# A graph layer on one core: node work on VectorE queued behind the turning of edges from block 24 on

## The chip, the cores and the metric

The kernel runs on one core of a Trainium2 chip. The core has a matmul engine (TensorE, PE in the profile, with its weight loads as PEld), VectorE (DVE), ScalarE (ACT), GpSimd (POOL) and SyncE (SP). Each engine works off its own queue in order, and they wait for each other through semaphores. The metric is the time of one execution on the device in microseconds, the median of several runs. Lower is better.

## The reference

The kernel computes one layer of a graph network over 8,192 nodes with 256 channels and 131,072 edges with 64 attributes each. Edges come sorted by their destination `dst`.

```python
ea = edge_attr @ w_e + b_e
msg = relu(x[src] + ea)                       # one row of x gathered for every edge
agg = segment_sum(msg, dst, num_segments=N)
t = x + agg
h_local = bn1(relu(t @ w1 + b1) @ w2 + b2 + x)
# attention inside groups of 32 nodes, 4 heads of 64
h_attn = bn2(attention(x) @ out_w.T + out_b + x)
out = h_local + h_attn
out = bn3(out + relu(out @ m_w1 + m_b1) @ m_w2 + m_b2)
result = layernorm(x + out)
```

All arithmetic is in 32-bit floats.

## The kernel before

Edges are cut into 128 blocks of 1,024, nodes into 16 chunks of 512. A block takes these steps:

- `gather` has GpSimd fetch the block's rows of x in eight indirect transfers of 128 rows (L217, tile `xs`, six buffers). Six blocks take one of the eight from SyncE instead (`FETCHED`, tile `xf`). From block 20 on the rows come from `xb`, a copy of x with the edge bias added.
- `edge_transpose` (L288) turns the block's edge attributes on VectorE with a 32x32 transpose: `ea` to `eaT`. This is "the turning of edges". `eaT` has two buffers, so the turning for block b+2 can begin only when the matmuls of block b have read theirs.
- `edge_products` multiplies `eaT` by the edge weights into the PSUM tile `pe` (two buffers of two banks each).
- `edge_messages` adds `xs` to `pe` on VectorE (L348) and applies the relu on ScalarE (L352), both in `xs`. The additions wait for the gathers.
- `edge_hot` builds on VectorE the 0/1 matrix `oh` (L363) that says which destination each edge has.
- `pair_sums` or `some_sums` sum the messages by destination with matmuls into `pw`; `edge_sums` copies them to `ws` (ScalarE) and builds a second 0/1 matrix `oh2` (VectorE, L402); `edge_place` multiplies the two into `l` and adds the result to the nodes' `xT` (VectorE, L422).

The node work of a chunk comes from three generators. `attention_front` makes the queries and keys. `attention_back` makes the values (`vn`, L609), the scores, then the softmax on VectorE: `mx` (L635), the subtraction (L638), an exponential on ScalarE (L639), the sum `sm` (L642), its reciprocal (L643), the scaling (L645) and four transposes into `bd` (L649). Then come matmuls that read `bd`. `dense` does the two feed-forward parts with VectorE steps in `hA` (L672, L701) and `zT` (L719), then the final normalisation in `y`, `st`, `mv`, `rstd` (L732 to L744). The last chunks use `dense_rows` (L761 on).

What sets the order: TensorE's order is the order of the program text throughout (`manual_schedule`). VectorE's and ScalarE's are written out the same way up to block 24 (`NV`), where `stated[0]` becomes false. From then on the framework's scheduler orders these two by its own estimate of when each instruction is ready, and `tc.issue_after(ins)` adds one rule: what is traced inside it on the engine of `ins` stands behind `ins` in that engine's queue. It adds no wait for `ins` to finish. From block 104 (`TAIL`) on, the text is produced by a small planner with due times, and it takes blocks one by one.

The gathers run under `hold_fetches`: each gather also waits for a matmul that the plan puts about 10 us (`AHEAD`) before it, at 1.254 us for each gather.

In the kernel before, two functions queue their work behind the newest turning: the additions of `edge_messages` and the comparisons of `edge_hot`, by way of `turned_at`:

Of the kernel before, what the change touches and what calls it, by code (L numbers as in the profile page):

```python
# [12 lines left out]
AF = mybir.ActivationFunctionType  # L13
ALU = mybir.AluOpType
# [5 lines left out]
P = 128  # L20
N, C, E, ED, H, NPG = 8192, 256, 131072, 64, 4, 32
# [3 lines left out]
NB = E // BE  # L25
NH = 4
WN = P // NH
TJ = BE // NH // P
TB = NH * TJ
QR = 32  # L30
EQ = P // QR
# [12 lines left out]
FETCHED = [44, 54, 64, 76, 86, 98]  # L44
# [40 lines left out]
def gnn_kernel(ctx: ExitStack, tc: tile.TileContext, x, src, dst, edge_attr, w, out):  # L85
    nc = tc.nc
# [16 lines left out]
    iota_n = const.tile([P, WB], FP, name="iota_n")  # L103
# [15 lines left out]
    rel = const.tile([P, NB, TB], FP, name="rel")  # L119
# [14 lines left out]
    for v in VECS:  # L134
        n = w[v].shape[0] // P
# [92 lines left out]
    xf_of = {}  # L228
# [48 lines left out]
    stated = [True]  # L277

    def between():
        for do in spots:  # L280
            do()

    turned_at = [None]

    def edge_transpose(b):
        ea, g0 = ea_of[b // 2], b % 2 * NH * EQ
        eaT = eaT_of[b] = epool.tile([P, NH * EQ, QR], FP, name="eaT", tag="eaT", bufs=2)
        turned_at[0] = nc.vector.transpose(eaT, ea[:, QR:].rearrange("p (g d) -> p g d", d=ED)[:, g0 : g0 + NH * EQ, :QR]).ins  # L288


    pe_of, msg_of, oh_of, pw_of, newest = {}, {}, {}, {}, {}
# [21 lines left out]
    def next_edges(b):  # L313
        if b < NB:
            edge_transpose(b)
        ahead = 2 + (b >= 24)
        while loaded[0] < min(b + ahead, NB - 1):
            loaded[0] += 1
            load_edges(loaded[0])
        fetch_rows(b - 2)  # L320

    def edge_messages(b, pairs=range(0, NH, 2), of_pair=range(2)):

        xs = xs_of[b]
        if b not in msg_of:
            msg_of[b] = xs
        msg = msg_of[b]
        n = 2 if b < NB - 1 else 1
        with ExitStack() as behind:
            if not stated[0]:  # L330
                behind.enter_context(tc.issue_after(turned_at[0]))
            for h in pairs:
                pe = pe_of[b, h]
                for u in of_pair[::n]:
                    hs = slice(h + u, h + u + n)
                    if h + u + n == NH and b in FETCHED:
                        for us, js, rows in (
                            (slice(0, 2), slice(0, TJ - 1), xs[:, h:]), (slice(0, 1), slice(TJ - 1, TJ), xs[:, h:]),
                            (slice(1, 2), slice(TJ - 1, TJ), xf_of[b]),
                        ):  # L340
                            rows = rows[:, None, None, :] if rows is xf_of[b] else rows[:, us, js].rearrange("p u i c -> p i u c")
                            nc.vector.tensor_add(
                                msg[:, h:][:, us, js].rearrange("p u i c -> p i u c"), pe[:, js, us, :], rows
                            )
                        nc.scalar.activation(msg[:, hs], msg[:, hs], AF.Relu)
                        continue
                    for js in [slice(0, TJ)] if n == 2 or h + u < NH - 1 else [slice(j, j + 1) for j in range(TJ)]:
                        nc.vector.tensor_add(  # L348
                            msg[:, hs, js].rearrange("p u i c -> p i u c"), pe[:, js, u : u + n, :],
                            xs[:, hs, js].rearrange("p u i c -> p i u c"),  # L350
                        )
                        nc.scalar.activation(msg[:, hs, js], msg[:, hs, js], AF.Relu)  # L352
        between()

    def edge_hot(b):

        oh = oh_of[b] = epool.tile([P, TB, WN], FP, name="oh", tag="oh", bufs=2)
        with ExitStack() as behind:
            if not stated[0]:
                behind.enter_context(tc.issue_after(turned_at[0]))  # L360
            for t0 in range(0, TB, TB // 2):
                ts = slice(t0, t0 + TB // 2)
                nc.vector.tensor_tensor(  # L363
                    oh[:, ts],
                    iota_n[:, None, :WN].to_broadcast([P, TB // 2, WN]),
                    rel[:, b, ts, None].to_broadcast([P, TB // 2, WN]),
                    ALU.is_equal,
                )

    def group_sums(pw, i, b, turns):  # L370
        for h, j in turns:
# [58 lines left out]
    with tc.tile_pool(name="setup", bufs=1) as sp:  # L430
# [16 lines left out]
        for v in VECS:  # L447
            r, n = col[v]
# [14 lines left out]
        for b in range(2):  # L463
            edge_transpose(b)
            load_edges(b + 2)
# [3 lines left out]
        edge_products(0, (2,))  # L469
        next_edges(2)  # L470
        edge_messages(0)


# [450 lines left out]
    with tc.manual_schedule(engines={PE}):  # L924
# [39 lines left out]
        for i, c, a, z in (  # L964
# [20 lines left out]
        b = 0  # L985
        while b < TAIL:
# [24 lines left out]
            if stated[0]:  # L1011
                for h in range(0, NH, 2) if b else ():
                    edge_products(b, (h,))
                    edge_messages(b, (h,))
# [17 lines left out]
                copy_some(2)  # L1032
# [6 lines left out]
            else:  # L1039
# [24 lines left out]
        p, m = [b, 0], [b, 0]  # L1064
# [10 lines left out]
        while l < NB:  # L1075
# [56 lines left out]
            elif t >= times[2]:  # L1132
                i, k = p
# [17 lines left out]
    with tc.If(wide > 0):  # L1151
        with tc.tile_pool(name="gen", bufs=1) as pool, tc.tile_pool(name="gen_ps", bufs=1, space=PSUM) as ps_pool:
# [11 lines left out]
            with tc.For_i(0, E, P * TE) as e0:  # L1164
                ea = pool.tile([P, TE, ED], FP, name="gea")
# [7 lines left out]
                xs = pool.tile([P, TE, C], FP, name="gxs")  # L1173
# [7 lines left out]
                for j in range(TE):  # L1181
# [89 lines left out]
```

## Time and profile before

| what | value |
|---|---|
| median of three runs | 1311.12 us (1310.87 to 1316.0) |
| profiled execution: time, span | 1310.63 us, 1308.9 us |
| granted TensorE clock in it | 0.966 |
| busy: PE, DVE, ACT, POOL | 1200.1, 792.5, 581.6, 971.1 us |
| turnings of edges, 128x512 | 128, 701 ns each |
| additions 128x1024 | 248, 1217 ns each |
| transposes into `bd`, 32x512 | 64, 701 ns each |

A row of the timeline view gives start, length, engine, line, operation, tiles, form and count; in brackets how long the engine stood idle before it, and what ended that. A row of the windows view gives the stretch, its length, the busy time of each engine shown with the number of its instructions, the granted TensorE clock, the share of the transfer engines and GB/s.

### The profile page before, as it was taken

What the parts mean: (1) busy time and instruction counts of PE and PEld (TensorE: products, weight loads), DVE (VectorE), ACT (ScalarE), POOL (GpSimd) and SP (SyncE); (2) the same over time, 40 slices, a digit from 0 to 9 for tenths busy, and PEclk for the clock granted to TensorE, in tenths of its full rate; (3) what the DMA queues carried; (4) which work ended last, traced back from release to release, by engine and by line L of the source; (5) the groups of instructions that cost most, each with busy time, mean ns of one, the idle gap of its engine ahead of it and who ended that gap; (6) DMA issues with size and microseconds to landing.
All of it is one profiled execution on the core that took longest, in us unless ns stands there. A gap on an engine that the chain in (4) does not pass through costs nothing.

```text
span 1308.9 us, 23368 instructions
## 1 busy us (share of the span) xinstructions
PE 1200.1 (92%) x7671; PEld 722.8 (55%) x7671; DVE 792.5 (61%) x1643; ACT 581.6 (44%) x840; POOL 971.1 (74%) x1026
## 2 busy tenths in 40 slices
PE   4997999899979989798998979979889999999997
PEld 3564556555546545555555545545455655556576
DVE  6676856647446565474746638346565765666563
ACT  3443534445526354352544426425245544545343
POOL 6777777777777777777777777777777777777772
PEclk9998999999999989899999989989989999999999
DMA  8999987767768657667687765866777775777642
GB/s 235 290 298 331 285 218 171 166 174 172 187 151 202 155 152 183 163 159 184 155 187 182 175 167 145 190 162 175 183 186 170 189 182 138 202 160 183 150 133 62
DMA packets 146298, 240.53 MB, mean 184 GB/s; under 512 B 24606, under 2 KB 109756, under 8 KB 145404
## 3 DMA queue, kind: packets, MB, share of 16 engines
q0 software_dynamic: 48864, 133.50, 38.1%
q1 hardware_dynamic: 88828, 98.15, 32.4%
q10 hardware_dynamic: 8480, 7.35, 1.9%
q8 instruction: 62, 1.02, 0.3%
q14 instruction: 64, 0.52, 0.1%
HBM read 222.13 MB, written 16.78 MB: 183 GB/s over the span
## 4 chain that ended last, share of the span: by engine, by line
PE 76%; DMA 9%; issue 5%; DVE 4%; POOL 3%; ACT 1%; SPq 0%; DVEq 0%; POOLq 0%; ACTq 0%
PE at L174 38%; PE pe L174 20%; PE pw L174 9%; PE l L174 5%; DMA xs<-xb,srci 4%; POOL xs L217 3%; DVE xs L348 2%; DMA xn<-in_x_dram 2%; DMA xs<-in_x_dram,srci 1%; PE at L775 1%; PE at L178 1%; DMA ea<-in_edge_attr_dram 1%; PE at L726 1%; ACT xs L352 1%; DMA last_src<-in_src_dram 0%
## 5 line engine op out<-in xcount | busy, mean ns | idle before, releaser
L217 POOL DMA_INDIRECT xs<-xb,srci x858 | 815.4, 950 | 262.3 <-issue 181.4
L352 ACT ACTIVATE xs<-xs 128x1024 f32<-128x1024 f32 (+2 forms) x253 | 263.0, 1045 | 434.0 <-DVE xs L348 357.8
L348 DVE TENSOR_TENSOR xs<-pe,xs 128x1024 f32<-128x1024 f32 (+2 forms) x253 | 300.0, 1204 | 211.1 <-PE pe L174 105.4
L174 PE MATMUL pe<-we,eaT 64*128 64x256 f32 x2048 | 271.1, 401 | 10.1 <-DVE xs L348 8.7
L174 PEld LDWEIGHTS pe<-we,eaT 64*128 64x128 f32 x2048 | 196.1, 194 | 108.5 <-issue 66.3
L174 PE MATMUL pw<-xs,oh 128*32 128x256 f32 x2048 | 142.9, 395 | 32.4 <-issue 20.2
L217 POOL DMA_INDIRECT xs<-in_x_dram,srci x144 | 138.6, 962 | 45.2 <-issue 29.3
L174 PEld LDWEIGHTS pw<-xs,oh 128*32 128x32 f32 x2048 | 61.0, 111 | 113.7 <-issue 54.1
L174 PE MATMUL at<-xT,inT 128*128 128x512 f32 x256 | 121.2, 600 | 1.9 <-ACT xT L578 1.9
L174 PE MATMUL at<-hA,mw 128*128 128x512 f32 (+1 forms) x256 | 114.4, 573 | 0.0
L288 DVE STREAM_TRANSPOSE eaT<-ea 128x512 f32<-128x512 f32 x128 | 89.6, 701 | 36.2 <-PE pe L174 31.4
L174 PE MATMUL at<-m,mw 128*128 128x512 f32 (+1 forms) x256 | 108.9, 570 | 0.0
L174 PEld LDWEIGHTS l<-oh,ws 128*128 128x128 f32 x512 | 74.7, 197 | 20.3 <-issue 16.4
L422 DVE TENSOR_TENSOR xT<-l,xT 128x352 f32<-128x352 f32 (+14 forms) x107 | 43.2, 427 | 70.4 <-PE l L174 70.3
L174 PE MATMUL l<-oh,ws 128*128 128x160 f32 (+4 forms) x512 | 85.8, 308 | 0.0
L174 PEld LDWEIGHTS at<-xT,inT 128*128 128x128 f32 x256 | 47.0, 190 | 60.5 <-issue 50.5
L174 PEld LDWEIGHTS at<-m,mw 128*128 128x128 f32 x256 | 47.0, 190 | 46.5 <-issue 42.2
L707 ACT ACTIVATE m<-at,vec 128x512 f32<-128x512 f32 (+1 forms) x64 | 41.8, 655 | 66.3 <-PE at L174 66.2
L174 PEld LDWEIGHTS at<-hA,mw 128*128 128x128 f32 x256 | 46.1, 190 | 44.0 <-issue 41.0
L591 ACT ACTIVATE qk<-at,vec 128x512 f32<-128x512 f32 x64 | 43.8, 685 | 52.9 <-PE at L174 52.5
L174 PE MATMUL pe<-qk 64*128 64x128 f32 x512 | 42.3, 321 | 23.2 <-DVE xs L348 23.2
L174 PE MATMUL at<-oT,outT 128*128 128x512 f32 x128 | 61.5, 604 | 0.3 <-ACT oT L664 0.3
(157 smaller groups left out, 1282.6 us busy)
## 6 DMA issues: line engine op xcount, KB each, us to landing
ea<-in_edge_attr_dram SPq DMA_DIRECT2D x252, 256.0 KB
xs<-xb,srci POOLq DMA_INDIRECT x858
xf<-xb SPq DMA_DIRECT2D x768, 1.0 KB
xn<-in_x_dram ACTq DMA_DIRECT2D x14, 512.0 KB
out_dram<-y SPq DMA_DIRECT2D x14, 512.0 KB
xp<-in_x_dram SPq DMA_DIRECT2D x10, 512.0 KB
xb<-xp SPq DMA_DIRECT2D x10, 512.0 KB
xp<-in_x_dram SPq DMA_DIRECT2D x3, 1024.0 KB
```

Source lines behind the costliest of these rows:

```text
L174: mark(ps, nc.tensor.matmul(ps, *args, **kw).ins)
L178: ins = nc.tensor.transpose(ps, *args).ins
L217: nc.gpsimd.indirect_dma_start(out=xs[:, h, j, :], out_offset=None, in_=x if b < NX else xb[:, :], in_offset=bass.IndirectOffsetOnAxis(ap= ...
L288: turned_at[0] = nc.vector.transpose(eaT, ea[:, QR:].rearrange("p (g d) -> p g d", d=ED)[:, g0 : g0 + NH * EQ, :QR]).ins
L348: nc.vector.tensor_add(msg[:, hs, js].rearrange("p u i c -> p i u c"), pe[:, js, u : u + n, :], xs[:, hs, js].rearrange("p u i c -> p i u c"),
L352: nc.scalar.activation(msg[:, hs, js], msg[:, hs, js], AF.Relu)
L422: newest["xT"] = nc.vector.tensor_add(xT, l2[:, :, a - n : z - n], xT).ins
L591: nc.scalar.activation(qk[:, o, :], ps, AF.Identity, bias=v_("in_b", o))
L707: newest["relu"] = nc.scalar.activation(m1[:, o, :], layer(mw1, KC, o, hA), AF.Relu, bias=v_("m_b1", o)).ins
L726: nc.tensor.transpose(ps[:wt, t - t2, k * P : (k + 1) * P], zT[:, k, t * P : t * P + wt], ident)
L775: nc.tensor.matmul(ps[i], wt[:, k, o * P : (o + 1) * P], act[:, k, :], start=(k == 0), stop=(k == nk - 1))
```

## The change

`edge_transpose` now opens an `issue_after` context on its own instruction and leaves it open until the next turning is traced (the last block's turning opens none). All that is traced on VectorE between two turnings is queued behind the first: the comparisons and additions as before, and now `oh2`, `xT`, `hA`, `vn`, `zT`, the softmax and the normalisation too. The two inner contexts of `edge_messages` and `edge_hot` go away.

```diff
-    turned_at = [None]
+    behind_turn = ctx.enter_context(ExitStack())

     def edge_transpose(b):
         ea, g0 = ea_of[b // 2], b % 2 * NH * EQ
         eaT = eaT_of[b] = epool.tile([P, NH * EQ, QR], FP, name="eaT", tag="eaT", bufs=2)
-        turned_at[0] = nc.vector.transpose(eaT, ea[:, QR:]...).ins
+        ins = nc.vector.transpose(eaT, ea[:, QR:]...).ins
+        behind_turn.close()
+        if not stated[0] and b < NB - 1:
+            behind_turn.enter_context(tc.issue_after(ins))
...
     def edge_messages(b, pairs=range(0, NH, 2), of_pair=range(2)):
-        with ExitStack() as behind:
-            if not stated[0]:
-                behind.enter_context(tc.issue_after(turned_at[0]))
-            for h in pairs:
...
+        for h in pairs:
...
     def edge_hot(b):
-        with ExitStack() as behind:
-            if not stated[0]:
-                behind.enter_context(tc.issue_after(turned_at[0]))
-            for t0 in range(0, TB, TB // 2):
...
+        for t0 in range(0, TB, TB // 2):
```

No instruction is added or removed. The rows of PE, POOL and SP stand in the same order before and after; VectorE's rows move, and with them some of ScalarE's. The new file is three lines shorter above most of the code, so that its line numbers are three lower there.

The first place is VectorE's queue past block 104, at the softmax of the chunk before the last. Before, this stood there (`eaT` is a turning, the additions are `xs<-pe,xs`, `oh` alone are the comparisons, `oh` with a number is `oh2`):

```order
L719 TENSOR_TENSOR zT<-at,zT 128x512
L635 TENSOR_REDUCE mx<-pr 128x16
L638 TENSOR_TENSOR pr<-pr,mx 128x128 x4
L642 TENSOR_REDUCE sm<-pr 128x16
L719 TENSOR_TENSOR zT<-at,zT 128x512
L643 RECIPROCAL sm<-sm 128x16
L645 TENSOR_TENSOR pr<-pr,sm 128x128 x4
L649 STREAM_TRANSPOSE bd<-pr 32x16x32 x4
L288 STREAM_TRANSPOSE eaT<-ea 128x512
L363 TENSOR_TENSOR oh<-iota_n,rel 128x128 x2
L422 TENSOR_TENSOR xT<-l_10516,xT 128x2x144
L348 TENSOR_TENSOR xs<-pe,xs 128x2x2x256 x2
```

The whole softmax stood ahead of the turning. Now, at the same place of the same queue, where the normalisation of another chunk (`y`, `st`, `mv`) is met as well:

```order
L288 STREAM_TRANSPOSE eaT<-ea 128x512
L360 TENSOR_TENSOR oh<-iota_n,rel 128x128 x2
L419 TENSOR_TENSOR xT<-l_10516,xT 128x2x144
L348 TENSOR_TENSOR xs<-pe,xs 128x2x2x256 x2
L632 TENSOR_REDUCE mx<-pr 128x16
L729 TENSOR_TENSOR y<-at,xn 128x512
L635 TENSOR_TENSOR pr<-pr,mx 128x128 x4
L729 TENSOR_TENSOR y<-at,xn 128x512
L731 BN_STATS st<-y 128x6
L639 TENSOR_REDUCE sm<-pr 128x16
L732 BN_AGGR mv<-st 128x2
L731 BN_STATS st<-y 128x6
```

The softmax stands behind the turning, its comparisons, an addition to `xT` and two additions of messages, and it alternates with the normalisation; after these rows come the reciprocal, the scaling, two more `st` and two more `mv`, and then the four `bd<-pr`.

The second place is the softmax of the last chunk, some 60 us later in VectorE's queue. Before:

```order
L635 TENSOR_REDUCE mx<-pr 128x16
L638 TENSOR_TENSOR pr<-pr,mx 128x128 x4
L288 STREAM_TRANSPOSE eaT<-ea 128x512
L363 TENSOR_TENSOR oh<-iota_n,rel 128x128 x2
L422 TENSOR_TENSOR xT<-l_10987,xT 128x2x128
L348 TENSOR_TENSOR xs<-pe,xs 128x2x2x256 x2
L642 TENSOR_REDUCE sm<-pr 128x16
L719 TENSOR_TENSOR zT<-at,zT 128x512
L643 RECIPROCAL sm<-sm 128x16
L402 TENSOR_SCALAR oh_11042<-iota_n,wrow 128x128
L645 TENSOR_TENSOR pr<-pr,sm 128x128 x4
L649 STREAM_TRANSPOSE bd<-pr 32x16x32 x4
```

Its first half filled the time ahead of the turning. After the change, from the comparisons on:

```order
L360 TENSOR_TENSOR oh<-iota_n,rel 128x128 x2
L419 TENSOR_TENSOR xT<-l_10987,xT 128x2x128
L348 TENSOR_TENSOR xs<-pe,xs 128x2x2x256 x2
L632 TENSOR_REDUCE mx<-pr 128x16
L716 TENSOR_TENSOR zT<-at,zT 128x512
L635 TENSOR_TENSOR pr<-pr,mx 128x128 x4
L399 TENSOR_SCALAR oh_11042<-iota_n,wrow 128x128
L716 TENSOR_TENSOR zT<-at,zT 128x512
L639 TENSOR_REDUCE sm<-pr 128x16
L640 RECIPROCAL sm<-sm 128x16
L642 TENSOR_TENSOR pr<-pr,sm 128x128 x4
L646 STREAM_TRANSPOSE bd<-pr 32x16x32 x4
```

All of it stands behind the additions, and its second half also behind the second `zT`, which stood behind `bd` before.

The third place is another 60 us on, at a block's `oh2`, the tile `oh_11593`. Before, in VectorE's queue:

```order
L363 TENSOR_TENSOR oh<-iota_n,rel 128x128 x2
L402 TENSOR_SCALAR oh_11593<-iota_n,wrow 128x112
L732 TENSOR_TENSOR y<-at,xn 128x512
L764 TENSOR_TENSOR xc<-xn,c3row 128x256
L734 BN_STATS st<-y 128x6 x2
L735 BN_AGGR mv<-st 128x2
L288 STREAM_TRANSPOSE eaT<-ea 128x512
```

It was built ahead of the normalisation. After the change:

```order
L729 TENSOR_TENSOR y<-at,xn 128x512
L731 BN_STATS st<-y 128x6 x2
L732 BN_AGGR mv<-st 128x2 x2
L288 STREAM_TRANSPOSE eaT<-ea 128x512
L729 TENSOR_TENSOR y<-at,xn 128x512 x2
L731 BN_STATS st<-y 128x6 x2
L732 BN_AGGR mv<-st 128x2
L731 BN_STATS st<-y 128x6
L732 BN_AGGR mv<-st 128x2
L731 BN_STATS st<-y 128x6
L732 BN_AGGR mv<-st 128x2
L399 TENSOR_SCALAR oh_11593<-iota_n,wrow 128x112
```

`oh2` has gone behind a turning and most of the normalisation of two pieces. From block 24 to 103 the moves repeat once in eight blocks: `hA` and `zT` steps that stood ahead of a turning stand behind it, and comparisons come earlier against `xT`, `hA` and `oh2`.

More of the change, by code (lines that the diff above doesn't have):

```diff
@@ L328, in edge_messages @@
         n = 2 if b < NB - 1 else 1
-        with ExitStack() as behind:
-            if not stated[0]:
-                behind.enter_context(tc.issue_after(turned_at[0]))
-            for h in pairs:
[L333 to L347, printed above, removed]
@@ new lines, in edge_messages @@
+        for h in pairs:
+            pe = pe_of[b, h]
+            for u in of_pair[::n]:
+                hs = slice(h + u, h + u + n)
+                if h + u + n == NH and b in FETCHED:
+                    for us, js, rows in (
+                        (slice(0, 2), slice(0, TJ - 1), xs[:, h:]), (slice(0, 1), slice(TJ - 1, TJ), xs[:, h:]),
+                        (slice(1, 2), slice(TJ - 1, TJ), xf_of[b]),
+                    ):
+                        rows = rows[:, None, None, :] if rows is xf_of[b] else rows[:, us, js].rearrange("p u i c -> p i u c")
@@ L348, in edge_messages @@
                         nc.vector.tensor_add(
-                            msg[:, hs, js].rearrange("p u i c -> p i u c"), pe[:, js, u : u + n, :],
-                            xs[:, hs, js].rearrange("p u i c -> p i u c"),
-                        )
-                        nc.scalar.activation(msg[:, hs, js], msg[:, hs, js], AF.Relu)
+                            msg[:, h:][:, us, js].rearrange("p u i c -> p i u c"), pe[:, js, us, :], rows
+                        )
+                    nc.scalar.activation(msg[:, hs], msg[:, hs], AF.Relu)
@@ L353, in edge_messages @@
+                    continue
+                for js in [slice(0, TJ)] if n == 2 or h + u < NH - 1 else [slice(j, j + 1) for j in range(TJ)]:
+                    nc.vector.tensor_add(
+                        msg[:, hs, js].rearrange("p u i c -> p i u c"), pe[:, js, u : u + n, :],
+                        xs[:, hs, js].rearrange("p u i c -> p i u c"),
+                    )
+                    nc.scalar.activation(msg[:, hs, js], msg[:, hs, js], AF.Relu)
         between()
@@ L357, in edge_hot @@
         oh = oh_of[b] = epool.tile([P, TB, WN], FP, name="oh", tag="oh", bufs=2)
-        with ExitStack() as behind:
-            if not stated[0]:
-                behind.enter_context(tc.issue_after(turned_at[0]))
-            for t0 in range(0, TB, TB // 2):
[L362 to L368, printed above, removed]
+        for t0 in range(0, TB, TB // 2):
+            ts = slice(t0, t0 + TB // 2)
+            nc.vector.tensor_tensor(
+                oh[:, ts],
+                iota_n[:, None, :WN].to_broadcast([P, TB // 2, WN]),
+                rel[:, b, ts, None].to_broadcast([P, TB // 2, WN]),
+                ALU.is_equal,
+            )
     def group_sums(pw, i, b, turns):
```

2 lines of the change are left out of this document (1 added, 1 removed).

## The prediction

> **What bounds the kernel now.** I read the page first, then the timelines of GpSimd, TensorE and VectorE. The page's busy times, and its chain of work that ended last:
>
> ```profile
> PE 1200.1 (92%) x7671; PEld 722.8 (55%) x7671; DVE 792.5 (61%) x1643; ACT 581.6 (44%) x840; POOL 971.1 (74%) x1026
> PE 76%; DMA 9%; issue 5%; DVE 4%; POOL 3%; ACT 1%; SPq 0%; DVEq 0%; POOLq 0%; ACTq 0%
> ```
>
> TensorE looks like the bound, but GpSimd's timeline says who sets the pace for most of the span. The first and the last gather, and the largest wait of the gathers (waits view):
>
> ```profile
> 4.30 1.10 POOL L217 DMA_INDIRECT xs<-in_x_dram,srcd  x1 [2.70 <-issue]
> ...
> 1285.58 0.95 POOL L217 DMA_INDIRECT xs<-xb,srci  x1 [0.30 <-issue]
> POOL xs L217 <- issue: 217.1, 704, 2.7
> ```
>
> There are 8 x 128 - 6 = 1018 gathers, so (1285.58 - 4.30) / 1017 = 1.26 us from one to the next, of which a row shows 0.95 busy and 0.30 of issue. The longest idle time, 2.7 us, is that before the first. So GpSimd issues without a pause from 4.3 to 1286.5 us, and nothing TensorE or VectorE does makes that stream shorter. TensorE catches up with it in every chunk and waits. A wait of VectorE or TensorE therefore costs time only in two cases: it holds a gather back, or it comes so late that TensorE does not catch up again. From the last gather to the end of the span there are 1308.9 - 1286.5 = 22.4 us.
>
> An example of a catch-up in the middle, TensorE's and then VectorE's timeline:
>
> ```profile
> 851.07 3.60 PE L174 MATMUL at<-m,mw 128*128 128x512 f32 x8
> 859.62 2.07 PE L174 MATMUL pw<-xs,oh 128*32 128x256 f32 x16 [4.95 <-ACT xs L352]
> 859.27 0.45 DVE L363 TENSOR_TENSOR oh<-iota_n,rel 128x128 f32<-128x128 f32 x2
> ```
>
> The sums `pw` waited 4.95 us, and the comparisons `oh` started at 859.27, just ahead of them; in the new order they come behind the turning before.
>
> **Blocks 24 to 103.** There the moves repeat once in a chunk: a step in `hA` or `zT` (about 0.7 us) goes behind a turning (0.70 us), comparisons come earlier. The turning itself gets free of those steps. I cost it at nothing: what hides it is the gather stream, at 1.26 us a gather. If the cover were gone, one step behind one turning would cost 0.7 us for each of eight or nine chunks, about 6 us; if the earlier comparisons end waits like that of 4.95 us, TensorE gets ahead instead and waits for gathers. Either way the end does not move. No instruction of GpSimd's or SyncE's queue moves past another, so the transfers keep their order.
>
> **Past block 104 (about 1050 us on)** TensorE has hardly any idle time, so a wait stays in the end. Three places count.
>
> *Place 1, the softmax of the chunk before the last.* VectorE, then TensorE, with the work on the tile `pr` from 1104 to 1112 us (windows view) in the first row:
>
> ```profile
> 1104.00:1112.00 8.00, 5.97 (x14) 0.86 (x2) 1.00 0.39 109
> 1109.05 2.85 DVE L649 STREAM_TRANSPOSE bd<-pr 32x512 f32<-32x512 f32 x4
> 1111.93 0.71 DVE L288 STREAM_TRANSPOSE eaT<-ea 128x512 f32<-128x512 f32 x1
> ...
> 1115.56 1.28 DVE L732 TENSOR_TENSOR y<-at,xn 128x512 f32<-128x512 f32 x2
> ...
> 1118.28 0.68 DVE L288 STREAM_TRANSPOSE eaT<-ea 128x512 f32<-128x512 f32 x1
> 1106.65 2.00 PE L174 MATMUL pe<-we,eaT 64*128 64x256 f32 x16
> ...
> 1114.66 3.51 PE L174 MATMUL pe<-we,eaT 64*128 64x256 f32 x16 [2.73 <-DVE xs L348]
> 1118.09 1.07 PE L174 MATMUL pw<-xs,oh 128*32 128x256 f32 x16
> 1119.09 1.97 PE L174 MATMUL at<-bd,vn 128*64 128x128 f32 x32
> ```
>
> Before, the softmax was done at 1111.90 and TensorE read `bd` at 1119.09: 7.2 us of slack. Now the turning goes first. It needs the products to have read `eaT`, which ends at 1106.65 + 2.00 = 1108.65. Behind it come comparisons, `xT` and two additions: 1115.56 - 1111.93 = 3.63 us by the old rows. Then the softmax, 5.97 us on `pr` and about 0.24 for the reciprocal, and between its steps the normalisation up to the next turning: 1118.28 - 1115.56 = 2.72 us. Together 12.56 us, so `bd` is ready at 1121.2: TensorE is 2.1 us late if its own position is as before. It may be earlier. Without the wait of 4.95 us above TensorE should be ahead on its way into this part; every microsecond by which the products end sooner takes one off, as the gathers of that block have long landed. I take 0.5 us (the ends are 0.1 and 2.1), since the rows of the middle speak for a lead of over 1 us.
>
> *The clock.* TensorE then has nothing to do between `pw` and `at<-bd,vn`: the 2.73 us of idle before the second products and their slow run go, and it waits some 6 us in one piece. After the idle 2.73 us the same 16 products took 3.51 us instead of 2.00, 1.5 us more; after the idle 4.95 us above, 16 sums took 2.07 instead of 1.07, and 1.0 us is only the start of it. What this trace shows is thus that TensorE runs at half speed for some microseconds after a wait of about 2.7 us or more. The old dip is over by the time `bd` is read; the new one begins there. I take 2.2 us, with 1.0 and 3.0 as ends.
>
> [...]
>
> *Place 2, the last softmax.* VectorE, then TensorE:
>
> ```profile
> 1169.12 0.70 DVE L288 STREAM_TRANSPOSE eaT<-ea 128x512 f32<-128x512 f32 x1
> ...
> 1172.71 0.67 DVE L642 TENSOR_REDUCE sm<-pr 128x16 f32<-128x512 f32 x1
> 1173.30 0.67 DVE L719 TENSOR_TENSOR zT<-at,zT 128x512 f32<-128x512 f32 x1
> 1173.90 0.24 DVE L643 RECIPROCAL sm<-sm 128x16 f32<-128x16 f32 x1
> ...
> 1175.10 2.85 DVE L649 STREAM_TRANSPOSE bd<-pr 32x512 f32<-32x512 f32 x4
> 1166.63 2.08 PE L174 MATMUL pe<-we,eaT 64*128 64x256 f32 x13
> ...
> 1169.18 7.03 PE L174 MATMUL at<-m,mw 128*128 128x512 f32 x16
> ...
> 1179.71 1.97 PE L174 MATMUL at<-bd,vn 128*64 128x128 f32 x32
> ```
>
> The turning starts at 1166.63 + 2.08 = 1168.7 and the additions end 1172.71 - 1169.12 = 3.59 us later, at 1172.3. The first softmax steps fit before 1176.2, when TensorE gives the second `zT` its input (1169.18 + 7.03). From there VectorE has that `zT` 0.67, the sum 0.67, the reciprocal 0.24, the scaling about 0.9 (what the 5.97 us leave beside the transposes, two reductions and the equal subtraction) and `bd` 2.85: 5.3 us, to 1181.5. TensorE wants `bd` at 1179.71. That is 1.8 us, and it adds to what came before, since both the turning and `zT` wait for TensorE. The ends are 0.5, if `zT` is waited for less, and 2.5.
>
> *Place 3, `oh2` behind the normalisation:*
>
> ```profile
> 1240.64 0.27 DVE L402 TENSOR_SCALAR oh<-iota_n,wrow 128x112 f32<-128x112 f32 x1
> 1240.83 0.68 DVE L732 TENSOR_TENSOR y<-at,xn 128x512 f32<-128x512 f32 x1
> 1241.43 0.41 DVE L764 TENSOR_TENSOR xc<-xn,c3row 128x256 f32<-128x256 f32 x1
> ...
> 1245.78 0.16 DVE L735 BATCH_NORM_AGGREGATE mv<-st 128x2 f32<-128x6 f32 x1
> 1244.53 0.59 PE L174 MATMUL l<-oh,ws 128*128 128x112 f32 x4
> 1246.40 0.71 PE L775 MATMUL at<-xT,w 128*128 128x128 f32 x4 [1.28 <-DVE xT L422]
> ```
>
> The steps from 1240.83 to 1245.78, less `xc` (0.41, which now comes later), take 4.5 us. `oh2` then starts at 1245.2 and is done at 1245.4, where `l` wanted it at 1244.53: 0.9 us. Part of that comes back, because the matmul after `l` waited 1.28 us for `xT` anyway; but `xc` and two `y` steps now stand ahead of that `xT`. I take 0.9, ends 0 and 1.5.
>
> **Sum.** 0 + 0.5 + 2.2 + 1.8 + 0.9 = 5.4 us. The profiled execution took 1310.63 us (span 1308.9 and 1.7 around it), so 1316.0 against itself; the median of the runs, 1311.12, is 0.5 above, so the forecast for a median is 1316.5 us, 0.4% slower. All low ends give 1.6 us, all high ends 9.1.
>
> **Rivals.** *A, no change:* VectorE is busy 61%, and 7.2 us of slack swallow place 1 when TensorE comes early and its clock stays up; then places 2 and 3 at their low to middle values leave 0 to 2.5 us: 1312.5. For it speaks the lead out of the middle; against it that TensorE idles in one piece before `bd`, however early it is.
>
> *B, clearly slower:* no lead (2.1), the full dip (3.0), and a second dip after the wait at place 2, by the 1.5 us of the row at 1114.66: 2.1 + 3.0 + 1.8 + 1.5 + 0.9 = 9.3, so 1320.4. For it speaks that the wait at place 2 comes near 2 us; against it that this is still short of the 2.73 us after which a dip is seen. A held gather would end on this side too, should TensorE fall about 10 us behind its plan.
>
> *C, faster:* the new order takes away the idle 2.73 us at 1114.66 and the 1.5 us of slow products behind it, and TensorE brings up to 2 us of lead with it: 6.2 us less, 1304.9. It decides at place 1: `bd` would have to be ready at 1119.1 - 2.7 - 1.5 = 1114.9, where I have 1119 to 1121. A softmax that keeps 12.6 us behind a turning cannot.
>
> *That nothing is moved* is excluded: the orders of VectorE differ as shown.
>
> **How the numbers follow.** The forecast has 0.52, A 0.23, B 0.21, C 0.04. Half a per cent, about what a measurement here can tell from no change, is 6.6 us: 1304.6 to 1317.7. Of the forecast's 0.52 I put 0.10 past 1317.7, of B 0.20; of C 0.02 below 1304.6. So faster 0.02, slower 0.30, the same 0.68. The range 1311.5 to 1321 leaves out C, the best tenth of A and the worst third of B, together about 0.15.
>
> **What would show it.** In the trace after: GpSimd still at 1.26 us a gather to 1286; TensorE idle 5 to 7 us before the `at<-bd,vn` near 1120 with the rows behind at half clock, 1 to 2.5 us before the one near 1182, about 1 before the `l` near 1246; the waits of `pw` near 860 and 940 shorter or gone. I am wrong if gathers show gaps, if TensorE enters 1100 us later than before, or if the waits near 1120 are there and the end stays.

## The result and the profile after

The changed kernel takes 1319.9 us (median of six runs, 1316.78 to 1322.89), the kernel before 1311.78 us in the same set (six runs, 1309.82 to 1316.0). The ratio is 1.0058, with a 95% interval of 1.004 to 1.0076: 7.6 us slower (5.2 to 10.0). The profiled execution took 1316.78 us with a span of 1315.0, which is 6.1 us more than the span before. Ratios below are always against the kernel before in the same set of runs, because that kernel itself took 1585 and 1601 us in two of the sets.

The page of the changed kernel, busy times and the chain that ended last:

```profile
PE 1200.0 (91%) x7671; PEld 721.8 (55%) x7671; DVE 793.0 (60%) x1643; ACT 581.6 (44%) x840; POOL 970.7 (74%) x1026
PE 67%; DMA 14%; issue 8%; DVE 6%; POOL 4%; ACT 1%; SPq 0%; DVEq 0%; POOLq 0%; ACTq 0%
```

The engines work as long as before (TensorE 1200.0 us against 1200.1). Summed over the span, the 6.1 us is thus idle time of TensorE; where half clock appears at one place, it went at another. GpSimd's timeline of the changed kernel, its first and last gather:

```profile
4.22 1.10 POOL L217 DMA_INDIRECT xs<-in_x_dram,srcd  x1 [2.62 <-issue]
...
1288.17 0.95 POOL L217 DMA_INDIRECT xs<-xb,srci  x1 [0.30 <-issue]
```

The pace is (1288.17 - 4.22) / 1017 = 1.26 us a gather, as before. Past 1120 us, though, a few gathers are held: GpSimd idles 0.95 us before the one at 1124.75, 0.70 at 1127.64 and 0.84 at 1276.91, in place of the usual 0.30, where the kernel before has no idle time over 0.45 us in that stretch. TensorE's timeline of the changed kernel at the three places:

```profile
1106.57 2.00 PE L174 MATMUL pe<-we,eaT 64*128 64x256 f32 x16
...
1111.78 2.00 PE L174 MATMUL pe<-we,eaT 64*128 64x256 f32 x16
1113.71 1.22 PE L174 MATMUL pw<-xs,oh 128*32 128x256 f32 x16
1120.78 3.68 PE L174 MATMUL at<-bd,vn 128*64 128x128 f32 x32 [5.86 <-DVE bd L646]
1124.39 0.77 PE L174 MATMUL l<-oh,ws 128*128 128x144 f32 x4
...
1184.71 1.97 PE L174 MATMUL at<-bd,vn 128*64 128x128 f32 x32 [1.91 <-DVE bd L646]
...
1248.81 1.13 PE L174 MATMUL at<-xT,w 128*128 128x256 f32 x4
1251.18 0.67 PE L174 MATMUL l<-oh,ws 128*128 128x112 f32 x4 [1.24 <-DVE rstd L739]
1252.56 0.71 PE L772 MATMUL at<-xT,w 128*128 128x128 f32 x4 [0.71 <-DVE xT L419]
```

Two rows of the same view of the kernel before, which the comparison needs beside those of the prediction:

```profile
1120.99 0.76 PE L174 MATMUL l<-oh,ws 128*128 128x144 f32 x4
...
1243.56 1.13 PE L174 MATMUL at<-xT,w 128*128 128x256 f32 x4
```

Read the starts against each other. The first products are level (1106.57 against 1106.65), so up to that point this execution has neither lost nor gained anything. The products that read `bd` start 1.69 us later (1120.78 against 1119.09) and take 3.68 us in place of 1.97. So `l` behind them is 3.40 us late. At the second softmax the delay is 5.00 us (1184.71 against 1179.71), at the `at<-xT,w` of place 3 it is 5.25 (1248.81 against 1243.56), behind the wait for `oh2` and `xT` 6.16 (1252.56 against 1246.40), and 6.1 at the end of the span. Nothing is given back after place 1 except some tenths.

The windows view of the changed kernel, TensorE alone (stretch, length, busy time with instructions, granted clock, share of the transfer engines, GB/s):

```profile
1110.50:1114.00 3.50, 3.50 (x26) 1.00 1.05 217
1114.00:1117.60 3.60, 0.93 (x16) 1.00 1.12 212
1117.60:1121.00 3.40, 0.22 (x2) 0.50 1.04 330
1121.00:1124.40 3.40, 3.40 (x33) 0.50 0.38 112
```

TensorE runs dry at 1114.9 us, the granted clock is 0.50 from about 1117.6 to 1124.4, and the second half of that lies on the 32 products. In the kernel before a dip lay some microseconds earlier, on products that had waited 2.73 us (0.51 from 1114.40 to 1117.80; they took 3.51 us).

VectorE's timeline of the changed kernel, first at place 1, then at places 2 and 3:

```profile
1108.62 0.71 DVE L288 STREAM_TRANSPOSE eaT<-ea 128x512 f32<-128x512 f32 x1 [2.18 <-PE pe L174]
...
1112.25 0.68 DVE L632 TENSOR_REDUCE mx<-pr 128x16 f32<-128x512 f32 x1
...
1117.90 2.83 DVE L646 STREAM_TRANSPOSE bd<-pr 32x512 f32<-32x512 f32 x4
...
1179.26 0.69 DVE L716 TENSOR_TENSOR zT<-at,zT 128x512 f32<-128x512 f32 x1 [1.58 <-PE at L174]
...
1181.80 2.85 DVE L646 STREAM_TRANSPOSE bd<-pr 32x512 f32<-32x512 f32 x4
...
1250.79 0.24 DVE L399 TENSOR_SCALAR oh<-iota_n,wrow 128x112 f32<-128x112 f32 x1
```

The turning waits for TensorE until 1108.62, the softmax starts behind it at 1112.25, and `bd` is done at 1120.73. At place 2 the second `zT` waits for TensorE with the sum, the scaling and `bd` behind it, as the prediction's working had it.

### The profile page after: what moved, and what is told of

Its sections match the earlier page's. It is cut to its first block, busy times and chain, and to the rows that moved or that the text cites. A ratio compares the mean times of both kernels' runs of the same rounds, so it can differ in the third digit from the quotient of the medians.

```text
span 1315.0 us, 23353 instructions
## 1 busy us (share of the span) xinstructions
PE 1200.0 (91%) x7671; PEld 721.8 (55%) x7671; DVE 793.0 (60%) x1643; ACT 581.6 (44%) x840; POOL 970.7 (74%) x1026
## 4 chain that ended last, share of the span: by engine, by line
PE 67%; DMA 14%; issue 8%; DVE 6%; POOL 4%; ACT 1%; SPq 0%; DVEq 0%; POOLq 0%; ACTq 0%
PE at L174 34%; PE pe L174 17%; DMA xs<-xb,srci 10%; PE pw L174 8%; PE l L174 4%; POOL xs L217 4%; DVE xs L348 2%; DMA xn<-in_x_dram 1%; DMA xs<-in_x_dram,srci 1%; PE at L772 1%; DMA ea<-in_edge_attr_dram 1%; PE at L723 1%; PE at L178 1%; ACT xs L352 1%; DVE bd L646 0%
## 5 line engine op out<-in xcount | busy, mean ns | idle before, releaser
L174 PE MATMUL pe<-we,eaT 64*128 64x256 f32 x2048 | 264.5, 393 | 9.1 <-DVE xs L348 7.5
L174 PEld LDWEIGHTS pe<-we,eaT 64*128 64x128 f32 x2048 | 190.5, 189 | 105.9 <-issue 57.5
```

Source lines behind the costliest of these rows:

```text
L174: mark(ps, nc.tensor.matmul(ps, *args, **kw).ins)
```

## The experiments

The theory on trial: in blocks 24 to 103 the gathers hide what the rule moves, and the loss is made of three waits of TensorE and one stretch of half clock, all past block 104. The rivals: the loss arises in the middle, where the trace after shows more waiting for gathered rows; or it is the sum of many small moves in the tail, `oh2` above all; or the half clock has nothing to do with the wait.

Eight kernels ran first, in two sets of four. There the kernel before took 1584.95 us (first set) and 1601.13 us (second set), and the ratios are known to no better than 0.25%. Four more ran later, in sets in which it took 1313.02 and 1315.11 us.

| run | edit | kernel before, us | ratio, 95% interval | difference by the ratio, us |
|---|---|---|---|---|
| middle | new rule up to block 105 only | 1584.95 | 0.9944 (0.9917 to 0.997) | -8.9 |
| tail | new rule from block 106 on only | 1584.95 | 1.0023 (0.9996 to 1.005) | +3.6 |
| softmax_free | tail's softmax not behind the turning | 1584.95 | 0.9949 (0.9924 to 0.9975) | -8.1 |
| oh2_free | tail's `oh2` not behind the turning | 1584.95 | 0.9981 (0.9955 to 1.0006) | -3.0 |
| one_14 | before, with chunk 14's softmax behind the turning | 1601.13 | 1.0023 (0.9999 to 1.0047) | +3.7 |
| one_15 | before, with chunk 15's softmax behind the turning | 1601.13 | 1.0008 (0.9984 to 1.0031) | +1.3 |
| bd_14 | before, with chunk 14's `bd` alone behind it | 1601.13 | 0.9999 (0.9973 to 1.0025) | -0.2 |
| fill_wait | after, with 20 products in the wait | 1601.13 | 1.0028 (1.0002 to 1.0054) | +4.5 |
| middle_2 | as middle | 1313.02 | 1.0007 (0.9995 to 1.0019) | +0.9 |
| softmax_free_2 | as softmax_free | 1315.11 | 1.0011 (1.0001 to 1.0021) | +1.4 |
| one_14_2 | as one_14 | 1315.11 | 1.0021 (1.0007 to 1.0035) | +2.8 |
| fill_5 | after, with 10 products in the wait | 1315.11 | 1.0044 (1.0028 to 1.006) | +5.8 |

### The rule in the middle alone, and in the tail alone

The new rule stays for some turnings, and for the others the old one (additions and comparisons behind the newest turning) is put back:

```diff
-        if not stated[0] and b < NB - 1:
+        turned_at[0], opened[0] = ins, not stated[0] and b < NB - 1 and (b < 106)
+        if opened[0]:
             behind_turn.enter_context(tc.issue_after(ins))
...
+    def also_behind(stack, when):
+        if when and not stated[0]:
+            stack.enter_context(tc.issue_after(turned_at[0]))
...
+        with ExitStack() as behind:
+            also_behind(behind, not opened[0])
             for h in pairs:
```

`tail` has `b >= 106` in that place.

> The new rule only behind the turnings of blocks 24 to 105; from block 106 on the old one (additions and comparisons alone). Theory of the prediction (in blocks 24 to 103 the gathers hide what the rule moves, the loss arises past block 104): within 1.5 us of the kernel before, ratio 1.000 (0.999 to 1.0012), and the products of chunk 14's softmax (at<-bd,vn, x32) start near 1119 again, with no half clock behind them. Rival (the loss arises in the middle, because the trace of after shows more waiting for gathered rows there): 5 to 8 us slower than before, as the whole change.

> The old rule up to block 105, the new one only behind the turnings of blocks 106 to 126. Theory of the prediction: all of the loss is here, 5 to 8 us slower than before, ratio 1.004 to 1.006, and at<-bd,vn of chunk 14 starts 1 to 2 us later than in before with about 6 us of waiting ahead of it. Rival (the loss arises in the middle): within 1.5 us of before.

> The same kernel as in the run middle (the new rule only behind the turnings of blocks 24 to 105), again, because the kernel before took 1585 us there in place of 1312 and the new rule in the middle gained 9 us in that condition. If the gain belongs to the kernel at its usual pace too, 4 to 9 us faster than before (ratio 0.993 to 0.997), and the loss past block 104 would have to be 12 to 16 us. Theory of the prediction (the gathers hide the middle): ratio 0.999 to 1.0012. Rival (the loss arises in the middle): 1.004 to 1.006.

In the set where the kernel before took 1584.95 us, `middle` came out 8.9 us faster (4.8 to 13.2), which neither side had expected, and `tail` 3.6 us slower, with an interval that reaches past no change. The waits view of `middle` says what was different there. What the gathers waited for from TensorE, in total, times and longest:

```profile
POOL xs L217 <- PE at L174: 110.0, 91, 5.5
```

and the same row of the kernel before, in its own profile of 1310.63 us:

```profile
POOL xs L217 <- PE at L174: 19.1, 62, 0.5
```

In that set the gathers were held back by TensorE for up to 5.5 us at a time, and in `tail`, which has the old order in the middle, GpSimd idled 506.1 us ahead of the gathers from `xb`, 84.1 of them until a product of TensorE in `at` (262.3 and 17.3 in the kernel before); so they did not set the pace all the way any more. There the new order gained time in the middle; that it gained because the gathers were held is an inference. Where the gathers run almost without a pause, in `middle_2`, the same kernel is 0.9 us slower (0.7 us faster to 2.5 slower). Its TensorE timeline has the kernel before's rows at place 1, the 2.74 us wait included, but some 3.2 us later (1122.32 against 1119.09 for the products that read `bd`):

```profile
1117.83 3.56 PE L174 MATMUL pe<-we,eaT 64*128 64x256 f32 x16 [2.74 <-DVE xs L366]
...
1122.32 1.97 PE L174 MATMUL at<-bd,vn 128*64 128x128 f32 x32
```

So where the gathers set the pace the middle is neutral within that interval, as the prediction said, and the loss of 7.6 us does not arise there; a cost of up to 2.5 us is not excluded. The local effect of `tail` could be read in spite of the set: in its trace the products of chunk 14's softmax waited and then ran at half speed, and in that of `middle` they did not.

```profile
1366.15 3.68 PE L174 MATMUL at<-bd,vn 128*64 128x128 f32 x32 [4.19 <-DVE bd L666]
```

### Softmax or `oh2` out of the rule

In the tail the open context is closed around one group of steps and opened again behind it:

```diff
+    @contextmanager
+    def not_behind(when):
+        again = when and opened[0]
+        if again:
+            behind_turn.close()
+        yield
+        if again:
+            behind_turn.enter_context(tc.issue_after(turned_at[0]))
...
+        with not_behind(tail[0]):
             mx = pool.tile([P, TN * H], FP, name="mx", tag="mx")
...
+        with not_behind(tail[0]):
             sm = pool.tile([P, TN * H], FP, name="sm", tag="sm")
```

`oh2_free` has the same context around the `tensor_scalar` that builds `oh2`.

> As after, but past the last stated item (the tail) the steps of the softmax are not queued behind the turning, so that VectorE takes both of the tail's softmaxes where before took them. Theory of the prediction (places 1 and 2 and the clock dip carry all but 0.9 to 1.7 us): 0.5 to 2 us slower than before, 5 to 7 us faster than after. Rival (the loss is many small moves of the tail, of which the softmax is one): still 4 us or more slower than before.

> As after, but in the tail the scaling of the comparisons (oh2, in the edge sums) is not queued behind the turning. Theory of the prediction (oh2 costs only place 3, 0.9 to 1.7 us): 5 to 7 us slower than before, about 1 us faster than after. Rival (oh2 behind the turnings delays the pw products all along the tail): 0 to 2.5 us slower than before.

> The same kernel as in the run softmax_free (as after, but in the tail the softmax steps are not queued behind the turning), on a chip where the kernel before takes 1313 us. Theory of the prediction (places 1 and 2 and the clock dip carry the loss, place 3 alone is left): 0.5 to 2 us slower than before, ratio 1.0004 to 1.0015. Rival (many small moves of the tail): 4 us or more slower, 1.003 and up.

In the first set the 8.1 us by which `softmax_free` was faster and the 3.0 us of `oh2_free` both hold the gain in the middle, so that neither tests the tail by itself. Their difference does: the softmax out of the rule is 5.1 us better than `oh2` out of it, with intervals that still overlap by 0.2%. In the trace of `oh2_free` the products of chunk 14 still wait and run at half speed:

```profile
1356.31 3.68 PE L174 MATMUL at<-bd,vn 128*64 128x128 f32 x32 [5.05 <-DVE bd L667]
```

`softmax_free_2`, where the kernel before took 1315.11 us, is 1.4 us slower than it (0.1 to 2.8), within the 0.5 to 2 us expected. That is 6.2 us less than the loss of the change, with each ratio from a set of its own. Its TensorE timeline:

```profile
1114.98 2.00 PE L174 MATMUL pe<-we,eaT 64*128 64x256 f32 x16
...
1123.00 3.46 PE L174 MATMUL pe<-we,eaT 64*128 64x256 f32 x16 [2.75 <-DVE xs L366]
...
1127.40 1.97 PE L174 MATMUL at<-bd,vn 128*64 128x128 f32 x32
...
1254.56 0.67 PE L174 MATMUL l<-oh,ws 128*128 128x112 f32 x4 [1.33 <-DVE rstd L761]
```

At place 1 it has the kernel before's rows again: the wait of 2.75 us and the slow run stand ahead of the second products, and the products that read `bd` neither wait nor run slowly. The wait of place 3 is still there. The many small moves of the tail are thus worth little. The two softmaxes carry most of the loss.

### One softmax at a time

The kernel before, with one chunk's softmax steps queued behind the newest turning:

```diff
+        with ExitStack() as behind:
+            also_behind(behind, st is chunk[14])
             mx = pool.tile([P, TN * H], FP, name="mx", tag="mx")
...
+        with ExitStack() as behind:
+            also_behind(behind, st is chunk[14])
             sm = pool.tile([P, TN * H], FP, name="sm", tag="sm")
```

`one_15` has `chunk[15]`.

> The kernel before, with the softmax of chunk 14 alone queued behind the newest turning (place 1 alone). Theory of the prediction: the products at<-bd,vn x32 wait some 6 us, start 1 to 2 us later than in before, and half clock behind the wait costs 1.5 to 2.2 us more: 2.5 to 4 us slower than before. Rival (the wait only stands in for the one at 1114 in before, and what stands behind it has slack): within 1 us of before.

> The kernel before, with the softmax of chunk 15 alone queued behind the newest turning (place 2 alone). Theory of the prediction: a wait of 1 to 2.5 us ahead of at<-bd,vn x24 near 1182, too short for half clock, and 1.1 to 2.5 us slower than before. With chunk 14 alone (2.5 to 4) and place 3 (0.9 to 1.7) it should make up the whole loss of 5 to 8. Rival (it is given back to the gathers before the end): within 0.7 us of before.

> The same kernel as in the run one_14 (the kernel before, with chunk 14's softmax alone queued behind the newest turning). From the trace of after (1.7 us later at the products, 1.7 more behind them): 2.5 to 4 us slower than before, ratio 1.002 to 1.003, with a wait of 5 to 6 us ahead of at<-bd,vn x32 and 3.68 us for these products. Rival (what stands behind has slack): within 1 us of before.

In the set of 1601.13 us `one_14` and `one_15` gave +3.7 and +1.3 us, with intervals that include no change: of the expected size, but inconclusive by themselves. In the trace of `one_15` the expected wait of 1 to 2.5 us is not there: the last softmax's products waited 0.41 us for `bd` (at 1448.49) and took 3.43 us, while `bd_14` below, with the old order at that place, shows 3.55 us (at 1445.40) without any wait right ahead. Place 2 is thus not tested by itself at the usual pace. `one_14_2` is 2.8 us slower (0.9 to 4.6), and its TensorE timeline repeats that of the changed kernel to some hundredths of a microsecond up to `l`:

```profile
1120.80 3.68 PE L174 MATMUL at<-bd,vn 128*64 128x128 f32 x32 [5.85 <-DVE bd L670]
1124.41 0.81 PE L174 MATMUL l<-oh,ws 128*128 128x144 f32 x4
...
1182.78 1.97 PE L174 MATMUL at<-bd,vn 128*64 128x128 f32 x32
...
1249.47 0.71 PE L796 MATMUL at<-xT,w 128*128 128x128 f32 x4 [1.28 <-DVE xT L439]
```

This one softmax makes `l` 3.42 us late (1124.41 against 1120.99). At 1182.78 it is 3.07, at 1249.47 also 3.07, and the span is 1311.9, 3.0 us longer than before. Its row at 1182.78 is also the reference for the rest of the change: with the same past, the changed kernel is 1.93 us later at place 2 (1184.71 against 1182.78).

A variant asked whether the earlier turning could be had without the late `bd`, which is what rival C needs: only the four transposes into `bd` are queued behind it.

```diff
+        with ExitStack() as behind:
+            also_behind(behind, st is chunk[14])
             for g in range(GT):
                 q = slice(g * NPG, (g + 1) * NPG)
```

> The kernel before, with the four bd transposes of chunk 14 alone queued behind the turning, the rest of that softmax where before has it: the turning then comes earlier on VectorE, so that the 2.73 us wait of the pe products at 1114 and the slow run behind it should go, while bd is ready about when before has it. Rival C of the prediction (the wait and the slow products are worth 4 to 6 us): 3 to 6 us faster than before. Theory (l of the next sums then waits for its oh2, which stands behind the same work on VectorE, so that the lead is given back): within 1.5 us of before.

It gave 0.2 us less than the kernel before (4.3 less to 4.0 more), in the set of 1601.13 us. On TensorE:

```profile
1365.21 2.27 PE L174 MATMUL pe<-we,eaT 64*128 64x256 f32 x16 [1.97 <-DVE xs L366]
...
1370.53 1.97 PE L174 MATMUL at<-bd,vn 128*64 128x128 f32 x32
1373.19 0.73 PE L174 MATMUL l<-oh,ws 128*128 128x144 f32 x4 [0.69 <-DVE oh L419]
```

`bd` came in time, and `l` then waited 0.69 us for its `oh2`, as the theory had it. The wait of the products ahead did not go but stayed at 1.97 us. A gain of 3 to 6 us, by rival C, lies within the interval only at its lower edge. Whether this version gains a little where the gathers set the pace is open: it was not run there.

### Work in the wait

Products whose results are not used are put on TensorE in the wait ahead of chunk 14's `at<-bd,vn`, into the bank that these then overwrite:

```diff
             ps = bank()
+            if k == 0 and st is chunk[14]:
+                for _ in range(10):
+                    nc.tensor.matmul(ps, mw1[:, 0, :P], mw1[:, 0, :], start=True, stop=True, skip_group_check=True)
```

> As after, with ten more products of 128x512 (0.43 us each at their pace in after, 4.3 us together) on TensorE ahead of the at<-bd,vn of chunk 14, into the bank that these products then overwrite, so that the results are not used: the idle time there falls from 5.9 us to about 1.5. If the half clock behind the wait follows from the idle time, at<-bd,vn x32 takes about 2.0 us in place of 3.68 and l behind it starts 1.7 us earlier than in after: 1.3 to 2.2 us faster than after. If the half clock has another cause (or the fillers cost what they save): within 0.7 us of after.

Each written product became two instructions, so that the fillers took 8.85 us and not 4.3. They ran past the wait:

```profile
1361.02 8.85 PE L653 MATMUL at<-mw 128*128 128x512 f32 x20
1369.80 1.97 PE L174 MATMUL at<-bd,vn 128*64 128x128 f32 x32
```

The products took 1.97 us behind them, but the time (+4.5 us, in the set of 1601.13) says nothing on what that is worth. `fill_5` has `range(5)`:

> As fill_wait, with half as many extra products: in fill_wait they stood twice as many as meant (20 instructions, 8.85 us) and ran past the wait. Now 4.4 us of them in a wait of 5.9 us. If the half clock follows from the idle time: at<-bd,vn x32 takes 2.0 us and starts when it does in after (1.7 us later than in before), l behind it 1.7 us earlier than in after; the time 1 to 2.2 us under after's, 1.003 to 1.005 of before. If the half clock is not the idle time's: 3.68 us again, and after's time, 1.0058.

It is 5.8 us slower than the kernel before (3.7 to 7.9), in the expected range, but its interval overlaps with that of the change (5.2 to 10.0), so that the times alone do not separate the two. The trace does. TensorE's timeline:

```profile
1118.29 2.00 PE L174 MATMUL pe<-we,eaT 64*128 64x256 f32 x16
...
1121.37 4.56 PE L653 MATMUL at<-mw 128*128 128x512 f32 x10
1127.29 1.97 PE L174 MATMUL at<-bd,vn 128*64 128x128 f32 x32 [1.37 <-DVE bd L646]
1129.19 0.76 PE L174 MATMUL l<-oh,ws 128*128 128x144 f32 x4
...
1189.90 3.56 PE L174 MATMUL at<-bd,vn 128*64 128x128 f32 x32 [1.91 <-DVE bd L646]
```

From the second products to `l` it takes 1129.19 - 1118.29 = 10.90 us, where the changed kernel takes 1124.39 - 1111.78 = 12.61: 1.71 us less, all of it in the products that are no longer at half speed (1.97 against 3.68). In all five traces in which these products wait and nothing fills the wait (4.19 to 5.86 us: the changed kernel, `tail`, `oh2_free`, `one_14`, `one_14_2`) they take 3.68 us; in both with the fillers they take 1.97. So, as far as seven traces can say, the half clock at place 1 follows from the idle time. In this execution part of it came back at place 2, of which more at the end.

## Why the prediction was right, and where it was not

The forecast was 1316.5 us, 0.4% slower, with 1311.5 to 1321 as the range; the median is 1319.9, and the kernel is 0.58% slower. The mechanism and the three places are the forecast's. The sizes, by its terms:

| term | forecast, us | measured, us | from |
|---|---|---|---|
| blocks 24 to 103 | 0 | 0 in the trace (0.08 earlier, within place 1); +0.9 (-0.7 to 2.5) in `middle_2` | 1106.57 against 1106.65 |
| place 1, the wait | 0.5 (0.1 to 2.1) | 1.69 | 1120.78 against 1119.09 |
| the clock | 2.2 (1.0 to 3.0) | 1.71 | 3.68 against 1.97, and `fill_5` |
| place 2 | 1.8 (0.5 to 2.5) | 1.93 | 1184.71 against 1182.78 in `one_14_2` |
| place 3 | 0.9 (0 to 1.5) | 0.91 | 3.75 against 2.84 between the two `at<-xT,w` |
| given back or added between | 0 | -0.1 | the rest |
| sum | 5.4 | 6.1 | span 1315.0 against 1308.9 |

The sum of the traces came close partly by luck: the wait was 1.19 us larger than forecast and the clock 0.49 smaller, and the two misses have opposite signs. Against the median the forecast is 3.4 us short: 0.7 of it are the terms above, 0.7 the kernel before, whose median was 1311.78 in this set and not 1311.12, and 2.0 are open.

**The middle.** Right: the gathers kept 1.26 us, and TensorE reached place 1 at the same time. The last gather came 2.6 us later than before, but 2.3 of that arose past 1120 us, where gathers were held, by the view mostly by TensorE: a result of place 1 and what follows, and not its cause. Rightly foreseen too: of the waits of 4.95 us of `pw` near 860 and 940, 0.75 us are left of the first, at 856.15, and 1.27 of the second, at 935.07. What took their place are a wait of 2.83 us at 916.02 (1.51 before) and waits of the additions for gathered rows, in the waits view of the changed kernel:

```profile
DVE xs L348 <- DMA xs<-xb,srci: 156.6, 54, 8.9
```

where the kernel before has 76.3 us in 29 waits.

**Place 1, the step that failed.** `bd` was worked out to be ready at 1121.2 and was read at 1120.78, so the sum of the steps on VectorE held. What failed is the lead: "I take 0.5 us ..., since the rows of the middle speak for a lead of over 1 us." TensorE brought 0.08 us with it. There had been a lead, and it did not last. TensorE of the kernel before, at the scores (`pe<-qk`) near 950 and at a row past 1060:

```profile
961.48 3.78 PE L174 MATMUL pe<-qk 64*128 64x128 f32 x32 [3.51 <-DVE xs L348]
...
1070.40 1.98 PE L174 MATMUL at<-oT,outT 128*128 128x512 f32 x4
```

The changed kernel, the same two rows of TensorE and then two additions on VectorE:

```profile
948.73 1.16 PE L174 MATMUL pe<-qk 64*128 64x128 f32 x16 [0.91 <-DVE xs L348]
...
1067.59 1.98 PE L174 MATMUL at<-oT,outT 128*128 128x512 f32 x4
1071.28 1.23 DVE L348 TENSOR_TENSOR xs<-pe,xs 128x1024 f32<-128x1024 f32 x1 [3.99 <-issue]
...
1090.55 1.23 DVE L348 TENSOR_TENSOR xs<-pe,xs 128x1024 f32<-128x1024 f32 x1 [3.52 <-issue]
```

TensorE was 12.75 us ahead near 950 and still 2.81 ahead at 1067.59. Then the two additions waited 3.99 and 3.52 us. The view names no releaser, but the products that they read had ended at 1064.2 and 1084.4, so that only the gathered rows were left to wait for (in the waits view above they are named, as `DMA xs<-xb,srci`, for 54 waits of the additions, the longest of 8.9 us); TensorE waits for the additions in turn (1.43 us at 1072.56), and at the scores of 1100 it is level (1099.96 against 1100.03). A lead out of the middle thus lasts only until TensorE needs rows that are not there yet. That was already the argument for costing the middle at nothing, and the same argument excludes a lead out of it. With no lead the working gave 2.1, near the 1.69 measured.

**The clock.** Right in kind, 0.5 us too large. The 2.2 us was the author's estimate; the trace has a granted clock of 0.50 from 1117.60 to 1124.40, with 0.22 us of work in the first half of that, and 1.71 us lost on the 32 products in the second (3.68 against 1.97).

**Places 2 and 3.** Right within 0.2 us, though both figures are differences between traces, and no run at the usual pace has one of these places alone. At place 2 the second `zT` waited 1.58 us for TensorE as described, and no half clock followed in this execution. At place 3 the wait of 1.24 us ends with `oh2`, which was done at 1251.03 (1250.79 + 0.24); the view names `rstd`, a step right behind it. The following wait for `xT` fell from 1.28 to 0.71 us, and the net is 0.91.

**The rivals.** A needed the lead, and fell with it. C: the idle 2.73 us and the slow products did go (the row at 1111.78 takes 2.00), but `bd` was done at 1120.73 and not by 1114.9, so the time stood in the next wait. B is right that no lead is left at place 1, and names held gathers; its 1320.4 us is nearer the median than the forecast. Its longer dip and its second dip are not in the trace of the changed kernel.

**What stays open.** The medians differ by 8.1 us, the two profiled executions by 6.1. The profiled execution after is the fastest of its six runs, and its level start at place 1 may be luck. The other profiles with the new order in the middle, from sets in which the kernel before took 1313 to 1315 us, have the first products of place 1 at 1109.81 (`middle_2`), 1113.09 (`fill_5`) and 1114.98 (`softmax_free_2`) in place of 1106.65; TensorE had waited 2.47 us for an addition at 1073.88 in the first and 3.93 us for messages at 1097.99 in the second. `one_14_2`, with the old order there, has them at 1106.59. Two of the three are the slowest executions of their kernels, and `middle_2` as a whole is only 0.9 us slower, so that what a late start costs is not settled. A second candidate for the 2.0 us left is another dip, of 1.6 us, as in `fill_5`; a third is a longer hold of the gathers: from 1112 to 1130 us GpSimd was busy for 11.38 us in that run, for 12.83 in the changed kernel. No run separates them.

## What to carry to other kernels

Where one engine's stream set the pace (here a gather every 1.26 us), the order of the others cost little (0.9 us in `middle_2`, -0.7 to 2.5), but a lead won there by removing waits lasted only until the next waits for that stream (12.75 us near 950, none at 1100); a lead must be argued against the stream that sets the pace, not against the wait that went. Where the slack ends, look for what a queue rule puts behind an instruction that itself waits: here a softmax with 7.2 us of slack was put behind a turning that waits for TensorE, and was 1.7 us late. And the longer wait at a new place (5.86 us) moved a stretch of half clock onto work that counts (3.68 us in place of 1.97), so the idle time ahead of products is worth reading together with their duration.

## What the runs showed of the hardware

Equal waits did not have equal effects on TensorE's clock. At place 2 both the changed kernel and `fill_5` waited 1.91 us. The 32 products then took 1.97 us in the one and 3.56 us in the other. One chunk ahead of place 1, the products that read `bd` waited 1.83 us in `middle` (at 1277.53) and took 1.97 us. The windows views, first of the changed kernel, then of `fill_5`:

```profile
1184.50:1188.00 3.50, 3.29 (x44) 1.00 0.41 116
```

```profile
1189.80:1193.20 3.40, 3.30 (x32) 0.50 0.36 98
```

So 1.91 us of waiting was followed by half clock once and not the other time. What decides between the two cases is not settled.

A second thing was not expected and has no explanation here: in the sets of 1585 and 1601 us the same kernel before ran a fifth longer. These two sets ran on other chips (11 and 6) than the later ones (10 and 4); whether the chip is the cause was not tried. The gathers took as long as ever (948 ns each in `middle`, 950 before), but TensorE paused inside groups of products without a wait that the profile shows, as in this row of `middle`:

```profile
1428.49 0.46 PE L174 MATMUL at<-bd,vn 128*64 128x128 f32 x4 [0.43 <-issue]
```

The ratio of one and the same kernel against the kernel before went from 0.9944 to 1.0007 between the two conditions. Here a change of about half a per cent had one sign in one condition and was within the noise in the other.
